# Attention of 16 heads: probabilities computed a second time with keys in rows, in place of transposes

## The chip, the core and the metric

The kernel runs on one core of a Trainium2 chip, in one launch. The metric is the device time of one execution in microseconds (us), as the median of several. The profile shown is one execution taken by the hardware profiler; its own time is given beside its span.

The engines are named as in the profile: PE (TensorE; PEld is its weight loads), DVE (VectorE), ACT (ScalarE), POOL (GpSimd), and SP, which only issues DMAs here. Matrix products write to PSUM, whose eight banks hold 512 float32 columns each.

## The reference

The input x has 32 sequences of 128 tokens with 128 features. Twelve residual layers follow each other, each with a layer normalization in front. The change concerns the fourth and the fifth. Both have 16 heads of 8 features. In the fourth, the keys and values are 8 features shared by all heads, and attention is causal. In the fifth, keys and values come from a context of the same shape, and a mask of 0 and 1 per key hides some keys.

```python
# fourth layer
latent = x @ Wc_down
q = (latent @ Wq_up).reshape(Bsz, Tlen, N_HEAD, HEAD_DIM)
kv = latent @ Wkv_up
k, v = (kv[..., :HEAD_DIM], kv[..., HEAD_DIM:])
att = jnp.einsum('bthd,bsd->bhts', q, k) * (1.0 / np.sqrt(HEAD_DIM))
att = jnp.where(causal[None, None], att, -jnp.inf)
att = jax.nn.softmax(att, axis=-1)
y = jnp.einsum('bhts,bsd->bthd', att, v).reshape(Bsz, Tlen, C)
return y @ Wc_proj

# fifth layer: q, k, v = query @ Wq.T + bq, keys @ Wk.T + bk, values @ Wv.T + bv, split into heads
energy = jnp.einsum('bhqd,bhkd->bhqk', q, k)
energy = jnp.where(mask[:, None, None, :] == 0, jnp.float32(-1e+20), energy)
attention = jax.nn.softmax(energy / np.sqrt(HEAD_DIM), axis=-1)
out = jnp.einsum('bhqk,bhkd->bhqd', attention, v)
return out.transpose(0, 2, 1, 3).reshape(N, Lq, EMBED) @ Wo.T + bo
```

## The kernel before

The 32 sequences are 8 groups (`G`) of 4 (`J`). All activations stay on the chip. The function `attention16` (line 502) runs the fourth and the fifth layer (`layer3`, line 1283, and `layer4`, line 1326) in one loop of rounds; a round n handles one sequence j of a group g, so the first 32 rounds are the causal layer and the next 32 the masked one. The same function is used once more for a later layer (`layer7`), which the change leaves as it is.

For one sequence the stages are these. `scores` forms, for all 16 heads, the products of queries and keys, with queries in the partitions (rows) and keys in the columns. A head has only 8 features, so four heads lie in each group of 32 rows, and `expand_keys` (line 477) holds keys spread over four column blocks with zeros in the other heads' features. Four products of 32 rows and 512 columns, one for each row group, fill four PSUM banks. The causal or mask term is added by further bf16 products: 16 small corner products in the causal layer, four in the masked one. DVE takes the maximum over the keys of each half (8 heads, 1024 columns), subtracts it for 12 of the heads, and ACT takes exponentials; four heads get the maximum as ACT's bias instead. `transposes` (line 558) turns the 16 blocks of 128 x 128 probabilities over on PE, four to a bank, and ACT copies each bank to SBUF, so that the keys lie in the partitions. `weighted` (line 569) multiplies them by the values and by ones (for the denominators), in 32 products of 32 output rows; DVE divides. After a group's four sequences `project` (line 640) applies the output matrix and adds the result to x.

PSUM is handed out under three tags of two buffers each: `two` (two banks each), `ps` (one bank) and `acc` (one bank). `scores` takes both `two` buffers, `transposes` takes `ps`, `weighted` takes `acc`. In SBUF the 1 MB tiles `bbig` (4 buffers) hold the probabilities before and after turning.

Beside the rounds of one group the inputs of the next one or two are made in steps (`step`, line 586, resumes the generator `before` of the layer): normalization by `normed` (statistics on DVE, the rest on POOL), transposes of its result (`turned_over`), and products for keys, queries and values. In the causal layer the keys and queries are made by `late`, at the end of a round. The spreading of keys in `expand_keys` is four POOL operations.

Within `run` the wrapper `Ordered` keeps PE, ACT and DVE in the order in which the program issues their instructions; POOL and the DMAs are placed by the scheduler. The order of a round before is:

```python
transposes(n, 0); e = scores(n + 1); transposes(n, 1); e(0)
step(g + 1)            # and step(g + 2) where j == 2
e(1)
weighted(n - 1)
# late() where it waits; project for a finished group
```

Of the kernel before, what the change touches and what calls it, by code (L numbers as in the profile page):

```python
# [10 lines left out]
F32 = mybir.dt.float32  # L11
BF16 = mybir.dt.bfloat16
I32 = mybir.dt.int32
# [8 lines left out]
CBLS = 4  # L22
HALF = B * S // 2
G = 8
# [30 lines left out]
def constants():  # L55

    p = np.arange(128)
    c = Columns()
    c.add("ident", np.eye(128))
    c.add("upper", (p[:, None] <= p[None, :]) * 1.0)  # L60
    c.add("causal", np.where(p[None, :] > p[:, None], NEG, 0.0))
    c.add("ones4", np.broadcast_to(np.repeat(np.eye(4), 8, 1).reshape(1, -1), (128, 128)))

    head = p // 32 * 8 + p % 8
    c.add("spread", (head[:, None] == np.arange(256)[None, :] // 8) * (p[:, None] % 32 // 8 == 1) * 1.0)
    c.add("count", np.broadcast_to(np.arange(40), (128, 40)))
    c.add("row", p[:, None] * 1.0)
    c.add("hm16", (p[:, None] // 8 == np.arange(16)[None, :]) * 1.0)
    c.add("n4", (p[:, None] % 32 // 8 == np.arange(4)[None, :]) * 1.0)
    c.add("m4", (p[:, None] // 32 == np.arange(4)[None, :]) * 1.0)  # L70
    k = p % 32

    c.add("means", (p[:, None] // 32 == p[None, :] // 32) * (k[:, None] <= k[None, :]) / (k[None, :] + 1.0))
    c.add("minus", -1.0 * (k[:, None] == 0))
    for e in (4, 8, 16):
        i = np.arange(e)
        c.add(f"tri{e}", np.broadcast_to(((i[None, :] < i[:, None]) * 1.0).reshape(1, -1), (128, e * e)))
    c.add("ones", np.ones((128, 128)))
    c.add("nhalf", np.full((128, 4), -0.5))
    return c  # L80


# [120 lines left out]
def program(ctx, tc, cols, x, ctxt, mask, drop, dfirst, dsmall, dwide, drows, dunits, dexperts, dconst, drel, dwq, out):  # L203
# [16 lines left out]
    def two(shape=(128, 2, 512)):  # L220

        return pp.tile(list(shape), F32, tag="two", name="two", bufs=2)
# [10 lines left out]
    def gmid(shape=(128, 512), dtype=F32):  # L233
        return mid.tile(list(shape), dtype, tag="gmid", name="gmid", bufs=10)
# [4 lines left out]
    def small(*shape):  # L239
        n = int(np.prod(shape))  # L240
        return sm.tile([128, *shape], F32, tag=f"s{n}", name="s", bufs=4 if n < 128 else 2)
# [6 lines left out]
    def mm(o, lhsT, rhs, start=True, stop=True):  # L248
        T.matmul(o, lhsT=lhsT, rhs=rhs, start=start, stop=stop)
# [22 lines left out]
            V.tensor_copy(o, p)  # L272


    cs = const.tile([128, cconst.n], F32, name="cs")
    K = {n: cconst.view(cs, n) for n in cconst.at}
    ident = K["ident"]
    xg = []
    for i in range(G):
        t = const.tile([128, J, D], F32, name=f"x{i}")  # L280
        SY.dma_start(out=t, in_=x[i * J : i * J + J].rearrange("b s d -> s b d"))
        xg.append(t)
        if i == 0:
            SY.dma_start(out=cs, in_=dconst)
            w0 = units.tile([128, cfirst.n], F32, tag="unit", name="w0")
            A.dma_start(out=w0, in_=dfirst)
            ww = const.tile([128, cwide.n], F32, name="ww")
            A.dma_start(out=ww, in_=dwide.to_broadcast([128, cwide.n]))
            wr = const.tile([1, crows.n], F32, name="wr")
            A.dma_start(out=wr, in_=drows)  # L290
# [18 lines left out]
    identb = const.tile([128, 128], BF16, name="identb")  # L309
    V.tensor_copy(identb, ident)  # L310

    acausal = const.tile([128, 64], BF16, name="acausal")
    V.tensor_copy(acausal, W0["acausal"])
    flip = const.tile([128, 128], BF16, name="flip")
# [162 lines left out]
    def expand_keys(w, src, bias=None):  # L477

        o = gbig((128, 4, 512))
        p, k = ps(), bmid()  # L480
        mm(p, w, src)
        if bias is None:
            A.copy(k, p)
        else:
            A.activation(k, p, AF.Identity, bias=bias)
        for n in range(4):
            P.tensor_scalar(o[:, n, :], k, K["n4"][:, n : n + 1], None, ALU.mult)
        return o
# [13 lines left out]
    def attention16(*layers):  # L502
# [108 lines left out]
        def go_round(n, others, then):  # L611
            g, j = n // J, n % J
            e = None
            if n < groups * J:
                transposes(n, 0)
            if n + 1 < groups * J:
                e = scores(n + 1)
            if n < groups * J:
                transposes(n, 1)
            if e:  # L620
                e(0)
            step(g + 1)
            if j == 2:
                step(g + 2)
            if g + 1 >= groups or (j == 3 and g + 2 == groups):
                next(then, None)
            if e:
                e(1)
            if 0 < n <= groups * J:
                weighted(n - 1)  # L630
            if g + 1 < groups and "late" in held[g + 1]:
                held[g + 1].pop("late")()
            next(others, None)
            if n > 1 and (n - 2) % J == J - 1:
                done = (n - 2) // J
                project(done % G, outs.pop(done), *layers[done // G][3:5])

        return lead(), run

    def project(i, yT, wo, bo):  # L640

        p = ps((128, J, 128))
        for j in range(J):
            mm(p[:, j, :], yT[:, j * 128 : (j + 1) * 128], wo)
        if bo is not None:
            P.tensor_tensor(xg[i], xg[i], bc(bo, 1, J), ALU.add)
        add_x(i, p)

    def linearT(w, src, bias=None, scale=1.0):

        p = ps()
        mm(p, w, src)
        o = gmid()
        if bias is not None:
            A.activation(o, p, AF.Identity, bias=bias, scale=scale)
        else:
            A.mul(o, p, scale)
        return o
# [623 lines left out]

    def layer3():

        rows, past = gmid((128, 4, 128)), sm.tile([128, 4, 128], BF16, tag="cbl", name="past", bufs=CBLS)
        _, at, n = cconst.at["causal"]
        for r in range(4):
            SY.dma_start(out=rows[32 * r : 32 * r + 32], in_=dconst[:, at : at + n].rearrange("(a p) k -> p a k", p=32))
        V.tensor_copy(past, rows)

        def extra(i, j, r):
            at = slice(32 * r, 32 * r + 32)
            return [(slice(32 * a, 32 * a + 32), identb[at, at], bc(past[at, a], 1, 4)) for a in range(4)]

        def before(i, h):
            xn = normed(i)
            yield
            xnT = turned_over(xn)
            yield
            p = ps()  # L1300
            mm(p[0:64, :], W["a1_down"], xnT)
            lat = gmid((64, 512))
            A.copy(lat, p[0:64, :])

            def late():
                h["k"] = expand_keys(W["a1_k"], lat)
                h["q"] = linearT(W["a1_q"], lat)

            if i:
                h["late"] = late  # L1310
            yield
            if i == 0:
                late()
            yield
            v = values_tile()
            pv, f = ps((128, J, 8)), small(J, 8)
            for j in range(J):
                mm(pv[:, j, :], lat[:, j * 128 : (j + 1) * 128], W["a1_v"])
            A.copy(f, pv)
            P.tensor_copy(diagonal(v)[:, 0:J], bc(f, 2, 4))  # L1320
            h["v"] = lambda j, r, n: flat(v[:, j, n])

        return before, 8**-0.5, extra, W["a1_o"], None, None, (1, 0, 0, 0)


    def layer4():
        masks = {}
        V.tensor_scalar(W["L1_xattn_bq"], W["L1_xattn_bq"], 8**-0.5, None, ALU.mult)

        def before(i, h):  # L1330
            mi = gmid((128, J * S), I32)
            SY.dma_start(out=mi, in_=mask[i * J : i * J + J].rearrange("b s -> (b s)").unsqueeze(0).to_broadcast([128, J * S]))
            xn = normed(i)
            yield
            mb = masks[i] = gmid((128, J * S), BF16)
            V.tensor_scalar(mb, mi, 0.0, -1e20, ALU.is_equal, ALU.mult)
            xnT = turned_over(xn)
            yield
            h["k"] = expand_keys(W["x1_Wk"], ctxT[i], W["x1_bk"])
            yield  # L1340
            h["q"] = linearT(W["x1_Wq"], xnT, W["L1_xattn_bq"], 8**-0.5)
            yield
            h["v"] = head_values(ctxT[i], W["x1_Wv"], WW["L1_xattn_bv"])

        def extra(i, j, r):
            row = slice(32 * r, 32 * r + 1)
            return [(slice(0, 128), onesb[row, :], bc(masks[i][row, j * S : (j + 1) * S], 1, 4))]

        return before, 1.0, extra, W["x1_Wo"], WW["L1_xattn_bo"], None, (1, 0, 0, 0)


    def layer5():
# [865 lines left out]
    lead2, run2 = layer2()  # L2218
    run1(rest0, lead2)
    load_units(6, 7)  # L2220
    lead3, run3 = attention16(layer3(), layer4())
    run2(lead3)
    lead5, run5, last6 = layer5()
    run3(iter(()), lead5)
# [39 lines left out]
```

## Time and profile before

| What | Value |
|---|---|
| Time, three runs | 2785.57, 2786.37, 2797.83 us; median 2786.37 |
| The profiled execution | 2801.5 us, span 2799.7 us, mean granted PE clock 0.939 |
| Busy shares of the span | PE 87%, DVE 74%, ACT 54%, POOL 34% |
| First scores of the causal layer, last of the masked one | start at 1028.7 and 1486.1 us |

The time column of the views counts from the start of the span. A group of instructions is named by engine, operation, the tile written and the tiles read (buffer numbers left out), and the shapes. All instructions pass through one helper, so they have one line number, and tiles tell them apart: `two<-gbig,gmid` are the score products of both layers, `ps<-cs,bbig` the transposes, `acc<-bbig,val` and `acc<-bbig,cs` the weighted sums and denominators, `two<-past,identb` the causal corners, `two<-gmid,onesb` the mask's products, `ps<-ws,...` and `ps<-xnT,ws` the projections. A float32 product is two instructions, a transpose is one. After the bar stand busy time and the mean of one; overlapping instructions count once in the busy time. "idle" is the time that the engine stood before them, and the arrow names what ended it.

### The profile page before, as it was taken

To read this page: it belongs to the slowest core of one execution; us is meant where nothing else is said; L and a number is where in the kernel's file an instruction comes from. 1 tells how busy PE (TensorE), PEld (TensorE's weight loads), DVE (VectorE), ACT (ScalarE), POOL (GpSimd) and SP (SyncE) were. 2 spreads that over 40 slices of the span, in tenths; PEclk is the share of its full clock that TensorE was granted. 3 is DMA by queue.
4 is the path that set the end of the run, shared out by engine and by line. 5 is a ranking of instruction groups with operands and counts; after the bars stand their busy time and mean duration, and the time that the engine had idled before them with its cause. 6 is when DMAs were issued, how large, how long until landed. Compare 5 with 4: busy or idle time off the path is not lost.

```text
span 2799.7 us, 56299 instructions
## 1 busy us (share of the span) xinstructions
PE 2434.1 (87%) x22929; PEld 1586.5 (57%) x22948; DVE 2081.3 (74%) x4091; ACT 1512.7 (54%) x3394; POOL 945.0 (34%) x977
## 2 busy tenths in 40 slices
PE   5988989999979999999997999988778999866664
PEld 3565667777744446666664444445555688444443
DVE  6978868878888867888887555558896525898993
ACT  4656544444422237777774454467884334566663
POOL 3534452232310214335552011133441454143432
PEclk8978899999999999999999999989998999988876
DMA  3000000000000010000000000000002357000000
GB/s 121 2 2 2 6 21 9 5 9 4 1 24 1 1 34 2 6 10 10 11 5 16 0 1 1 0 1 2 2 13 78 106 195 251 15 23 12 23 12 19
DMA packets 51045, 73.83 MB, mean 26 GB/s; under 512 B 3905, under 2 KB 41538, under 8 KB 50658
## 3 DMA queue, kind: packets, MB, share of 16 engines
q1 hardware_dynamic: 47728, 61.63, 6.9%
q0 software_dynamic: 2624, 5.40, 0.5%
q8 instruction: 181, 2.97, 0.4%
q10 hardware_dynamic: 434, 3.21, 0.3%
q14 instruction: 78, 0.64, 0.1%
HBM read 57.33 MB, written 12.89 MB: 25 GB/s over the span
## 4 chain that ended last, share of the span: by engine, by line
PE 56%; DVE 29%; ACT 8%; issue 4%; POOL 2%; DMA 1%; SPq 0%; DVEq 0%; ACTq 0%; POOLq 0%
PE ps L191 23%; PE two L191 17%; PE acc L191 15%; DVE bbig L191 11%; DVE s L191 8%; ACT bbig L191 4%; DVE gmid L191 4%; DVE bmid L191 3%; ACT bmid L191 1%; POOL xn L191 1%; ACT gmid L191 1%; DVE x L191 1%; ACT xn L191 1%; POOL s L191 1%; DMA ys<-yt,at 0%
## 5 line engine op out<-in xcount | busy, mean ns | idle before, releaser
L191 PE MATMUL ps<-cs,bbig 128*128 128x128 f32 x2208 | 336.8, 290 | 84.3 <-ACT bbig L191 31.9
L191 PEld LDWEIGHTS ps<-cs,bbig 128*128 128x128 f32 x2208 | 250.7, 146 | 196.7 <-ACT bbig L191 94.2
L191 ACT COPY bbig<-ps 128x512 f32<-128x512 f32 x418 | 227.5, 583 | 187.7 <-PE ps L191 187.5
L191 DVE TENSOR_REDUCE s<-two 128x8 f32<-128x1024 f32 (+1 forms) x192 | 234.0, 1219 | 72.8 <-PE two L191 71.5
L191 PE MATMUL two<-xnT,u 128*128 128x512 f32 x512 | 257.5, 603 | 12.1 <-ACT bmid L191 5.5
L191 DVE TENSOR_TENSOR bbig<-bbig 128x1024 f32<-128x1024 f32 (+3 forms) x234 | 246.4, 1093 | 11.2 <-ACT bbig L191 9.2
L191 PE MATMUL acc<-bmid,u 128*128 128x512 f32 x416 | 216.0, 606 | 15.4 <-DVE bmid L191 14.1
L191 ACT ACTIVATE bbig<-two,s 128x256 f32<-128x256 f32 (+1 forms) x512 | 189.8, 419 | 21.1 <-DVE s L191 17.5
L191 DVE TENSOR_TENSOR bmid<-bmid,ps 128x512 f32<-128x512 f32 x192 | 129.9, 683 | 90.2 <-ACT bmid L191 70.5
L191 POOL TENSOR_SCALAR gbig<-bmid,cs 128x512 f32<-128x512 f32 x96 | 148.5, 1563 | 142.5 <-ACT bmid L191 142.5
L191 POOL TENSOR_TENSOR s<-s,cs 128x4 f32<-128x4 f32 x112 | 127.8, 1142 | 172.6 <-DVE s L191 164.2
L191 PE MATMUL two<-gbig,gmid 32*128 32x512 f32 (+1 forms) x1248 | 183.9, 563 | 0.0
L191 ACT ACTIVATE bbig<-bbig 128x512 f32<-128x512 f32 (+1 forms) x160 | 128.2, 801 | 68.2 <-DVE bbig L191 67.9
L191 PEld LDWEIGHTS two<-xnT,u 128*128 128x128 f32 x512 | 90.4, 189 | 114.7 <-issue 53.6
L191 ACT ACTIVATE bmid<-two 128x512 f32<-128x512 f32 x92 | 54.9, 597 | 171.6 <-PE two L191 163.7
L191 ACT ACTIVATE bmid<-two,ws 128x512 f32<-128x512 f32 x128 | 85.1, 686 | 104.4 <-PE two L191 104.2
L191 POOL TENSOR_TENSOR x<-x,ww 128x512 f32<-128x512 f32 x64 | 89.0, 1391 | 142.0 <-ACT xn L191 83.3
L191 PEld LDWEIGHTS acc<-bmid,u 128*128 128x128 f32 x416 | 75.0, 192 | 103.1 <-DVE bmid L191 47.5
L191 POOL TENSOR_TENSOR bbig<-bbig,s 128x1024 f32<-128x1024 f32 x32 | 60.6, 1893 | 213.3 <-PE two L191 152.7
L191 ACT ACTIVATE bbig<-bbig,s 128x128 f32<-128x128 f32 x384 | 118.7, 388 | 24.4 <-DVE s L191 24.4
L191 POOL TENSOR_TENSOR x<-x,xn 128x512 f32<-128x512 f32 x24 | 32.8, 1368 | 290.1 <-DVE xn L191 264.5
L191 DVE TENSOR_TENSOR bbig<-two,s 128x512 f32<-128x512 f32 (+1 forms) x128 | 122.6, 958 | 8.6
(300 smaller groups left out, 5728.0 us busy)
## 6 DMA issues: line engine op xcount, KB each, us to landing
we<-in_experts SPq DMA_DIRECT2D x36, 768.0 KB
u<-in_units SPq DMA_DIRECT2D x9, 768.0 KB
gmid<-in_ctx SPq DMA_DIRECT2D x16, 256.0 KB
x<-in_x SPq DMA_DIRECT2D x8, 256.0 KB
gmid<-in_mask SPq DMA_DIRECT2D x8, 256.0 KB
ys<-bbig SPq DMA_DIRECT2D x2, 1024.0 KB
gmid<-ys SPq DMA_DIRECT2D x8, 256.0 KB
gmid<-in_drop SPq DMA_DIRECT2D x8, 256.0 KB
```

The lines of the kernel that those rows point to most:

```text
L191: d = self.made = f(*args, **kwargs)
```

## The change

A new function `attention16_turned` replaces `attention16` for these two layers.

- `scores` still forms the products with queries in rows, but only for the maximum. DVE writes the negative maximum as two bf16 parts (a high and a low one), four copies each, in a tile of 128 x 128.
- `turn_shift` turns that tile over with one bf16 product, and ACT copies it.
- `probabilities` forms the scores again with keys in rows. In the causal layer these are four products of 512 columns, with queries that are spread over four blocks (`qx`), and 16 corner products; in the masked layer 16 products of 128 columns. Sixteen further bf16 products with `pick16` add the shift of each head. The four banks come from one `two`, one `ps` and one `acc` buffer. Three ACT instructions take exponentials out of PSUM straight into the tile that `weighted` reads. The mask of the fifth layer is a bias for each partition (`hidden`) in that instruction.
- The subtraction, the exponentials in rows, the 16 transposes and their four copies per sequence are gone.
- The order of a round, and the point at which the steps of later groups are resumed, are new: scores two rounds ahead, probabilities one round ahead.
- In the causal layer `late` spreads both keys and queries, eight POOL operations in place of four.
- The constants in HBM hold the causal mask twice (also turned over), and they are no longer loaded with the other constants.

```diff
+    c.add("pick16", (p[:, None] % 16 == 4 * (p[:, None] // 32) + np.arange(4)[None, :]) * 1.0)
+    c.kept = c.n
+    c.add("causal", np.where(p[None, :] > p[:, None], NEG, 0.0))
+    c.add("causalT", np.where(p[None, :] < p[:, None], NEG, 0.0))
...
+    def attention16_turned(*layers):
+
+        held, shifts, turned, outs, ahead = {}, {}, {}, {}, {}
+        groups = len(layers) * G
+        last = groups * J
+
+        def scores(n):
+
+            g, j = n // J, n % J
+            extra = layers[g // G][2]
+            qT, keys = held[g]["q"], held[g]["k"]
+            cols_j = slice(j * 128, (j + 1) * 128)
+            halves = [two((128, 2, 4, 128)) for _ in range(2)]
+            terms = [extra(g % G, j, r) for r in range(4)]
+            for r in range(4):
+                rows = slice(32 * r, 32 * r + 32)
+                mm(halves[r // 2][:, r % 2], qT[rows, cols_j], keys[rows, :, cols_j], True, not terms[r])
+            for r in range(4):
+                for at, lhsT, rhs in terms[r]:
+                    mm(halves[r // 2][at, r % 2], lhsT, rhs, False, True)
+            m, parts = small(16), small(64).bitcast(BF16).rearrange("p (c k h) -> p c k h", c=4, k=2)
+            for half in range(2):
+                V.tensor_reduce(m[:, 8 * half : 8 * half + 8], halves[half].rearrange("p r n k -> p (r n) k"), AX.X, ALU.max)
+            V.tensor_scalar(parts[:, :, 0, :], bc(m, 1, 4), -1.0, None, ALU.mult)
+            V.scalar_tensor_tensor(parts[:, :, 1, :], bc(m, 1, 4), -1.0, parts[:, :, 0, :], ALU.mult, ALU.subtract)
+            shifts[n] = parts.rearrange("p c k h -> p (c k h)")
+
+        def turn_shift(n):
+            p = ps((128, 128))
+            mm(p, shifts[n], identb)
+            shifts[n] = small(64).bitcast(BF16)
+            A.copy(shifts[n], p)
+
+        def probabilities(n):
+
+            g, j = n // J, n % J
+            _, scale, _, _, _, extra, bias = layers[g // G]
+            qT, keys, shift = held[g]["q"], held[g]["k"], shifts.pop(n)
+            cols_j = slice(j * 128, (j + 1) * 128)
+            pr = turned[n] = bbig((128, 16, 128))
+            pair, third, fourth = two((128, 2, 4, 128)), ps((128, 4, 128)), acc((128, 4, 128))
+            quarters = [pair[:, 0], pair[:, 1], third, fourth]
+            rows = [slice(32 * r, 32 * r + 32) for r in range(4)]
+            for r in range(4):
+                if extra:
+                    mm(quarters[r], held[g]["kT"][rows[r], cols_j], held[g]["qx"][rows[r], :, cols_j], True, False)
+            for r in range(4):
+                for at, lhsT, rhs in extra(r) if extra else ():
+                    mm(quarters[r][at], lhsT, rhs, False, False)
+            for k in range(4):
+                for r in range(4):
+                    if not extra:
+                        mm(quarters[r][:, k], keys[rows[r], k, cols_j], qT[rows[r], cols_j], True, False)
+                for r in range(4):
+                    mm(quarters[r][:, k], pick16[rows[r], k : k + 1].to_broadcast([32, 128]), shift[rows[r], :], False, not extra or k == 3)
+            for heads, src in ((slice(0, 8), pair.rearrange("p r n q -> p (r n) q")), (slice(8, 12), third), (slice(12, 16), fourth)):
+                if bias is None:
+                    A.activation(pr[:, heads], src, AF.Exp, scale=scale)
+                else:
+                    A.activation(pr[:, heads], src, AF.Exp, bias=bias(g % G, j), scale=scale)
+
...
+        def lead():
+            for _ in range(4):
+                step(0)
+                yield
+            step(0)
+            step(1)
+            yield
+            scores(0)
+            step(1)
+            turn_shift(0)
+            yield
+            probabilities(0)
+            scores(1)
+            turn_shift(1)
+            yield
+
+        def run(others, then):
+            follow(T, A, V)
+            for n in range(last + 1):
+                go_round(n, others, then)
+            for _ in then:
+                pass
+            follow()
+
+        def go_round(n, others, then):
+            g, j = n // J, n % J
+            if n + 2 < last:
+                scores(n + 2)
+            if n and j == 0:
+                done = g - 1
+                project(done % G, outs.pop(done), *layers[done // G][3:5])
+            step(g + 1)
+            if j >= 2:
+                step(g + 2)
+            if n >= last - 6:
+                next(then, None)
+            if n + 1 < last:
+                probabilities(n + 1)
+            if n < last:
+                weighted(n)
+            if n + 2 < last:
+                turn_shift(n + 2)
+            if g + 1 < groups and "late" in held[g + 1]:
+                held[g + 1].pop("late")()
+            next(others, None)
 
         return lead(), run
 
...
 
     def layer3():
 
-        rows, past = gmid((128, 4, 128)), sm.tile([128, 4, 128], BF16, tag="cbl", name="past", bufs=CBLS)
-        _, at, n = cconst.at["causal"]
-        for r in range(4):
-            SY.dma_start(out=rows[32 * r : 32 * r + 32], in_=dconst[:, at : at + n].rearrange("(a p) k -> p a k", p=32))
-        V.tensor_copy(past, rows)
-
-        def extra(i, j, r):
+        pasts = []
+        for name in ("causal", "causalT"):
+            rows, past = gmid((128, 4, 128)), sm.tile([128, 4, 128], BF16, tag="cbl", name="past", bufs=CBLS)
+            _, at, n = cconst.at[name]
+            for r in range(4):
+                SY.dma_start(out=rows[32 * r : 32 * r + 32], in_=dconst[:, at : at + n].rearrange("(a p) k -> p a k", p=32))
+            V.tensor_copy(past, rows)
+            pasts.append(past)
+
+        def corners(past, r):
             at = slice(32 * r, 32 * r + 32)
             return [(slice(32 * a, 32 * a + 32), identb[at, at], bc(past[at, a], 1, 4)) for a in range(4)]
 
...
             A.copy(lat, p[0:64, :])
 
             def late():
-                h["k"] = expand_keys(W["a1_k"], lat)
+                h["kT"] = linearT(W["a1_k"], lat)
                 h["q"] = linearT(W["a1_q"], lat)
+                h["k"], h["qx"] = gbig((128, 4, 512)), bbig((128, 4, 512))
+                for o, src in ((h["k"], h["kT"]), (h["qx"], h["q"])):
+                    for n in range(4):
+                        P.tensor_scalar(o[:, n, :], src, K["n4"][:, n : n + 1], None, ALU.mult)
 
             if i:
                 h["late"] = late
...
             P.tensor_copy(diagonal(v)[:, 0:J], bc(f, 2, 4))
             h["v"] = lambda j, r, n: flat(v[:, j, n])
 
-        return before, 8**-0.5, extra, W["a1_o"], None, None, (1, 0, 0, 0)
+        return before, 8**-0.5, lambda i, j, r: corners(pasts[0], r), W["a1_o"], None, lambda r: corners(pasts[1], r), None
 
 
     def layer4():
         masks = {}
+        mi32, mb32 = small(128).bitcast(I32)[0:B], small(64).bitcast(BF16)[0:B]
+        SY.dma_start(out=mi32, in_=mask)
+        V.tensor_scalar(mb32, mi32, 0.0, -1e20, ALU.is_equal, ALU.mult)
+        p, hidden = ps((128, B)), const.tile([128, B], F32, name="hidden")
+        mm(p, mb32, identb[0:B, 0:B])
+        V.tensor_copy(hidden, p)
         V.tensor_scalar(W["L1_xattn_bq"], W["L1_xattn_bq"], 8**-0.5, None, ALU.mult)
 
         def before(i, h):
...
             row = slice(32 * r, 32 * r + 1)
             return [(slice(0, 128), onesb[row, :], bc(masks[i][row, j * S : (j + 1) * S], 1, 4))]
 
-        return before, 1.0, extra, W["x1_Wo"], WW["L1_xattn_bo"], None, (1, 0, 0, 0)
+        return before, 1.0, extra, W["x1_Wo"], WW["L1_xattn_bo"], None, lambda i, j: hidden[:, i * J + j : i * J + j + 1]
 
 
     def layer5():
...
     lead2, run2 = layer2()
     run1(rest0, lead2)
     load_units(6, 7)
-    lead3, run3 = attention16(layer3(), layer4())
+    lead3, run3 = attention16_turned(layer3(), layer4())
     run2(lead3)
     lead5, run5, last6 = layer5()
     run3(iter(()), lead5)
```

More of the change, by code (lines that the diff above doesn't have):

```diff
@@ L60, in constants @@
     c.add("upper", (p[:, None] <= p[None, :]) * 1.0)
-    c.add("causal", np.where(p[None, :] > p[:, None], NEG, 0.0))
     c.add("ones4", np.broadcast_to(np.repeat(np.eye(4), 8, 1).reshape(1, -1), (128, 128)))
@@ L272, in evac @@
             V.tensor_copy(o, p)
-    cs = const.tile([128, cconst.n], F32, name="cs")
-    K = {n: cconst.view(cs, n) for n in cconst.at}
+    cs = const.tile([128, cconst.kept], F32, name="cs")
+    K = {n: cconst.view(cs, n) for n in cconst.at if cconst.at[n][1] < cconst.kept}
     ident = K["ident"]
@@ L283, in program @@
         if i == 0:
-            SY.dma_start(out=cs, in_=dconst)
+            SY.dma_start(out=cs, in_=dconst[:, 0 : cconst.kept])
             w0 = units.tile([128, cfirst.n], F32, tag="unit", name="w0")
@@ L310, in program @@
     V.tensor_copy(identb, ident)
+    pick16 = const.tile([128, 4], BF16, name="pick16")
+    V.tensor_copy(pick16, K["pick16"])
     acausal = const.tile([128, 64], BF16, name="acausal")
@@ L636, in go_round, with weighted, step @@
                 project(done % G, outs.pop(done), *layers[done // G][3:5])
+        return lead(), run
+    def attention16_turned(*layers):
[52 more added lines that the diff above has]
+                    A.activation(pr[:, heads], src, AF.Exp, bias=bias(g % G, j), scale=scale)
+        def weighted(n):
+            g, j = n // J, n % J
+            values, prT = held[g]["v"], turned.pop(n)
+            if j == 0:
+                outs[g] = gmid()
+            yd = acc((128, 2, 128))
+            for side in range(2):
+                for k in range(4):
+                    for r in range(4):
+                        mm(yd[32 * r : 32 * r + 32, side], ones4[:, k * 32 : k * 32 + 32] if side else values(j, r, k),
+                           prT[:, 4 * r + k, :], k == 0, k == 3)
+            rec = small(128)
+            V.reciprocal(rec, yd[:, 1])
+            V.tensor_tensor(outs[g][:, j * 128 : (j + 1) * 128], yd[:, 0], rec, ALU.mult)
+            if j == J - 1:
+                held.pop(g)
+        def step(g):
+            if g < groups:
+                if g not in ahead:
+                    held[g] = {}
+                    ahead[g] = layers[g // G][0](g % G, held[g])
+                next(ahead[g], None)
+        def lead():
[21 more added lines that the diff above has]
+        def go_round(n, others, then):
+            g, j = n // J, n % J
+            if n + 2 < last:
[17 more added lines that the diff above has]
+            next(others, None)
@@ L1283, in layer3 @@
     def layer3():
-        rows, past = gmid((128, 4, 128)), sm.tile([128, 4, 128], BF16, tag="cbl", name="past", bufs=CBLS)
-        _, at, n = cconst.at["causal"]
-        for r in range(4):
-            SY.dma_start(out=rows[32 * r : 32 * r + 32], in_=dconst[:, at : at + n].rearrange("(a p) k -> p a k", p=32))
-        V.tensor_copy(past, rows)
-        def extra(i, j, r):
+        pasts = []
+        for name in ("causal", "causalT"):
+            rows, past = gmid((128, 4, 128)), sm.tile([128, 4, 128], BF16, tag="cbl", name="past", bufs=CBLS)
+            _, at, n = cconst.at[name]
+            for r in range(4):
+                SY.dma_start(out=rows[32 * r : 32 * r + 32], in_=dconst[:, at : at + n].rearrange("(a p) k -> p a k", p=32))
+            V.tensor_copy(past, rows)
+            pasts.append(past)
+        def corners(past, r):
             at = slice(32 * r, 32 * r + 32)
```

## The prediction

> **What bounds the kernel now.** First the page's head: the core's TensorE (PE) is busy for most of the span and no other engine comes near.
>
> ```profile
> span 2799.7 us, 56299 instructions
> PE 2434.1 (87%) x22929; PEld 1586.5 (57%) x22948; DVE 2081.3 (74%) x4091; ACT 1512.7 (54%) x3394; POOL 945.0 (34%) x977
> ```
>
> That is an average over twelve layers, so I looked at the changed layers alone. The starts of the score products in the timeline repeat every 4 rounds: 29.5 us per group in the causal layer, 27.9 us in the masked one. The windows over one such group each (columns: length, then busy us of PE, PEld, DVE, ACT, POOL, then clock) read:
>
> ```profile
> 1114.59:1144.12 29.53, 28.11 (x444) 18.64 (x443) 23.61 (x37) 21.29 (x45) 11.39 (x13) 1.00 0.01 2
> 1400.19:1428.08 27.89, 26.14 (x394) 18.16 (x393) 23.86 (x38) 21.32 (x44) 15.54 (x20) 1.00 0.02 7
> ```
>
> PE is busy 95% and 94%; DVE 80% and 86%, ACT 72% and 76%. The clock is granted in full. Next the chain that ended last, for one round of the masked layer:
>
> ```profile
> 1406.84 1.29 PE two L191 x12
> 1408.13 0.60 PE ps L191 x4
> 1408.76 0.59 ACT bbig L191
> 1409.35 0.04 issue
> 1409.39 1.16 PE ps L191 x8
> 1410.55 1.88 PE acc L191 x64
> 1412.43 1.02 PE ps L191 x8
> 1413.46 1.29 PE two L191 x12
> ```
>
> The round is PE's own queue: scores 1.29, eight transposes (part of them shown as 0.60, with an ACT copy of 0.59 that frees a bank), a projection of the next group 1.16, weighted sums 1.88, eight transposes 1.02. So only what changes on PE, or makes PE wait, counts.
>
> **What leaves.** The relevant groups, from the lists by shape of the masked layer (31 rounds) and, after the dots, of the causal one (28 rounds):
>
> ```profile
> L191 PE MATMUL ps<-cs,bbig 128*128 128x128 f32 x504 | 70.4, 280 | 5.1 <-ACT bbig L191 5.1
> L191 ACT COPY bbig<-ps 128x512 f32<-128x512 f32 x125 | 67.4, 584 | 31.3 <-PE ps L191 31.3
> L191 DVE TENSOR_TENSOR bbig<-two,s 128x1024 f32<-128x1024 f32 x31 | 37.9, 1224 | 1.1
> L191 PEld LDWEIGHTS two<-gbig,gmid 32*128 32x128 f32 x248 | 9.7, 182 | 5.2 <-issue 3.8 <-DVE gmid L191 1.2 <-DVE s L191 0.2
> L191 PEld LDWEIGHTS <-onesb 1*128 1x128 bf16 x124 | 3.5, 93 | 7.0 <-issue 7.0
> ...
> L191 PE MATMUL two<-past,identb 32*32 32x512 bf16 x448 | 12.2, 384 | 0.0
> ```
>
> Per round go 16 transposes (70.4/31 = 2.3 us of PE, plus about 0.2 of waiting for the copies), four ACT copies (2.2 us), DVE subtractions of 1024 and 512 columns (1.9 us). DVE and ACT get slack, which is worth nothing by itself; PE gets 2.4 us a round.
>
> **What PE gets instead.** Masked layer: 16 score products of 128 columns, two instructions each, so 32, in four row groups at once, and 16 bf16 picks of the shift. Rows of this size (transposes, projections) run at the pace of their weight loads, so I price them by the loads: 9.7/248 = 39 ns a load when four row groups overlap, 45 with a gap: 32 x 0.045 = 1.4 us. The picks: 3.5/124 = 28 ns, with a gap 31: 16 x 0.031 = 0.5. Together 1.9 us. Bounds: by pure streaming (scores of 512 columns take 1.07 us for the same columns) plus 0.2 for the picks, 1.3; with every item at 1.4 times my price, 2.6. The middle is nearest to the load rows. Causal layer: four products of 512 columns as in the first scores, 1.07; 16 corner products, 0.36 from start to start (12.2/28 = 0.44 busy); picks 0.5; sum 1.95, bounds 1.65 and 2.4. The product that turns the shift: one of 128 columns, 0.13 like a transpose. So on PE alone the exchange is 2.4 for 2.0: a gain of 0.4 us a round. It does not stay.
>
> [...]
>
> **The new wait.** PSUM has two `two` buffers. scores(n+2) takes both, and probabilities(n+1), behind it on PE, needs one back: PE must wait until DVE has reduced the first half. Rows for that:
>
> ```profile
> 1116.14 1.23 DVE L191 TENSOR_REDUCE s<-two 128x8 f32<-128x1024 f32 x1 [2.19 <-PE two L191]
> ...
> 1414.77 1.22 DVE L191 TENSOR_REDUCE s<-two 128x8 f32<-128x1024 f32 x1 [0.93 <-PE two L191]
> ```
>
> The scores before them began at 1114.59 and 1413.39, so the bank is free 1.55 + 1.23 + 0.07 = 2.85 us after the start of scores (causal), 2.7 (masked). PE has scores (1.43; 1.29) and that round's projection step to fill this. Weighted sums, 1.88, would have filled it but stand behind it. In the old order transposes stood there. ACT's exponentials (1.06 + two of 0.63) end under the weighted sums and the next scores, and DVE's reciprocal and product (1.25) under the next scores: no wait there.
>
> **Sum per group of four rounds.** What follows probabilities' start is P + 1.9 + 0.13: masked 3.9, causal 3.95.
> Rounds j=1 and 2: masked 2.7 + 3.9 = 6.6 each (a step of 1.1 fits in the wait; before, 6.6). Causal 2.85 + 3.95 = 6.8.
> Round j=0: project and a step, 1.05 each, end at 3.4 to 3.5; then probabilities wants a `ps` bank. Either the step's, copied by ACT at about 4.2, or project's, which DVE's add frees behind both reductions, two shift operations (0.2 each, like other small rows) and its own 0.69: about 5.0. Middle 4.6. Masked 4.6 + 3.9 = 8.5 (before 8.47). Causal: half of the scores run ahead (0.5 less) and `late` costs 1.98 as before: 4.6 + 3.45 + 2.0 = 10.05 (before 10.28).
> Round j=3: the transposes of the next input move one round closer to its normalization. POOL's rows:
>
> ```profile
> 1407.20 0.23 POOL L191 TENSOR_SCALAR s<-s 128x4 f32<-128x4 f32 x1 [1.58 <-DVE s L191]
> 1407.51 1.04 POOL L191 TENSOR_TENSOR s<-s,cs 128x4 f32<-128x4 f32 x1
> 1408.66 3.12 POOL L191 TENSOR_SCALAR xn<-x,s 128x128 f32<-128x128 f32 x4
> ...
> 1112.00 6.19 POOL L191 TENSOR_SCALAR gbig<-bmid,cs 128x512 f32<-128x512 f32 x4 [8.96 <-ACT bmid L191]
> ```
>
> From the first to the end of the third, 4.6 us. DVE's statistics start behind the shift operations, 4.3 into j=2, and end at 5.5; POOL ends at 10.1, that is 3.5 into j=3; transposes to 3.9, then 3.9: 7.8 (before 6.2). Causal: the second spread of four, 6.19 us more on POOL, starts behind the first (kT copied at 9.65 after the start of j=0) and ends at 22.05, 5.2 into j=2; with the values 6.0; normalization to 10.6, 3.8 into j=3; 4.2 + 3.95 = 8.15 (before 6.4). The first spread ends at 15.9, before scores of the next group at 16.85, so it hides, with 1 us to spare.
> Masked: 6.6 + 6.6 + 8.5 + 7.8 = 29.5 against 27.9, +1.6; times 8 is +13. Causal: 6.8 + 6.8 + 10.05 + 8.15 = 31.8 against 29.5, +2.3; times 8 is +18. Start and end: the second scores can follow the first sooner, about 2 us (the old first round stood 3.4 us for exponentials), and one drain round goes, about 2: -4. The additional setup (four 64 KB DMAs, a mask DMA, a cast of 0.43, some small operations) is queued near 770 us, where the cast of the first mask ran at 774.6 under another layer's PE work: 0, or 1 to 2 if uncovered. SP has no other change in the loop.
> Total 13 + 18 - 4 = +27 us: the profiled execution would go from 2801.5 to 2828; it lies 15 above the median of 2786.4, and on the median I get 2813.
>
> **Rivals.**
> Slower, forecast: waits and moved steps take back more than PE's exchange gives, 2813.
> Faster: PE's queue alone counts. If a bank comes back in time (the scheduler's allocation, a prompter DVE) and P is at its low end, masked gives 2.4 - 1.3 - 0.13 = 1.0 a round, causal 2.4 - 1.65 - 0.13 = 0.6: 32 x 1.6 + 4 = 55, so 2731. It decides where PE shows no wait on DVE before probabilities, that is below 1.4 us of uncovered reduction. Against it: the reduction rows end 1.4 us after PE is through its scores. Half of that gain, 2759, would count here too.
> No change: low prices (1.3; 1.65) and the early `ps` bank, with the waits: three of four rounds shorten by 0.6 and 0.3, j=0 by 0.4: masked -2.2, causal -1.3 per group, 8 x 3.5 = 28 off: 2785.
> Much slower: 128-column loads do not overlap. By the transposes' load row (107 ns), 48 loads take 5.1 us: +3.2 x 32 = 102 in the masked layer, 2915.
>
> **How the numbers follow.** A measurement of this kernel tells 0.5% (14 us) from no change. Forecast 0.60, faster 0.13, no change 0.22, much slower 0.05. Low end: between 2759 and 2785, since the faster rival is cut, 2766. High end: prices 2.6 and 2.4 add 3 x 0.7 + 3 x 0.45 = 3.45 a group, 28; the late bank 0.45 x 16 = 7: 2848, and 2852 with the setup uncovered.
>
> **What would show it.** Right: before probabilities, PE idle behind DVE `s` (the reduction) in j=1 and 2 of the causal layer, about 1.4 us, and behind POOL `xn` in j=3; groups of about 31.8 and 29.5 us; ACT under 55% and DVE under 70% busy there, PE under 90%. Wrong: groups shorter than 29.5 and 27.9 with PE above 94% (the waits are hidden); or PE still full and longer (then the price of the 128-column products was too low).

## The result

| Kernel | Median | Runs |
|---|---|---|
| before | 2788.49 us | 2785.57 to 2797.83 |
| changed | 2831.42 us | 2829.93 to 2835.53 |

The ratio is 1.015, with a 95% interval of 1.0123 to 1.0178: the change makes the kernel 43 us slower by the medians. The profiled executions differ by less, 34.0 us in span (2833.7 against 2799.7), because the one of before lies 13 us above its median and the one of the changed kernel 4 us. The first product of the later layer's positions (`ps<-rels,flip`) starts at 1613.0 us instead of 1576.7, 36.3 us later, so the whole loss arises ahead of it, in the two changed layers.

The head of the changed kernel's page; the columns are as before:

```profile
span 2833.7 us, 59541 instructions
PE 2457.0 (87%) x24805; PEld 1571.3 (55%) x24805; DVE 2002.6 (71%) x4031; ACT 1362.0 (48%) x3008; POOL 999.8 (35%) x1009
```

DVE lost 79 us of work and ACT 151 us, and nothing was won by it. The windows over one group of each layer (length, then PE, PEld, DVE, ACT, POOL, clock):

```profile
1112.45:1143.81 31.36, 28.18 (x543) 15.28 (x542) 18.23 (x34) 11.58 (x22) 17.52 (x16) 1.00 0.01 2
1402.63:1433.38 30.75, 28.11 (x525) 19.55 (x524) 18.51 (x35) 12.36 (x21) 15.68 (x20) 0.89 0.04 11
```

The causal group takes 31.36 us (29.53 before), with nearly the same busy time of PE (28.18 and 28.11). The masked one takes 30.75 (27.89 before), and there the granted clock is 0.89 and no longer 1.00. The chain that ended last, over the rounds j=1 and j=3 of a masked group, shows both waits:

```profile
1402.70 1.33 PE two L194 x12
1404.03 1.22 DVE s L194
1405.29 0.38 PE two L194 x2
...
1406.84 1.89 PE acc L194 x65
...
1410.23 2.35 DVE s L194 x2
1412.60 0.43 DVE s L194
1413.05 1.49 DVE s L194 x9
...
1416.09 3.14 POOL xn L194 x4
1419.27 0.48 PE ps L194
...
1422.51 3.12 PE acc L194 x65
```

In j=1 DVE's reduction (`DVE s`, 1.22) now stands in the chain between the scores and the second scores. From j=2 into j=3 the chain leaves PE for 9 us (1410.23 to 1419.27): reductions, shift operations and statistics on DVE, then normalization on POOL. And the weighted sums behind that take 3.12 us where they took 1.89 before. The clock in windows of a few us around that place says why:

```profile
1411.40:1414.80 3.40, 3.31 (x112) 3.02 (x112) 3.06 (x12) 2.28 (x4) 1.88 (x5) 1.00 0.01 2
1414.80:1418.20 3.40, 2.24 (x23) 0.80 (x15) 3.04 (x4) 0.70 (x2) 3.21 (x5) 1.00 0.02 5
1418.19:1425.02 6.83, 6.22 (x100) 5.07 (x104) 1.33 (x4) 2.86 (x4) 3.43 (x5) 0.50 0.00 0
1425.00:1426.00 1.00, 1.00 (x29) 0.72 (x21) 0.29 (x1) 0.17 (x1) 0.00 (x1) 0.99 0.08 16
```

After a stretch in which PE was busy for 2.24 of 3.40 us, the clock falls to 0.50 and stays there from 1418.19 to 1425.02. In the causal layer, whose wait is the same kind:

```profile
1125.26 0.70 PE L194 MATMUL two<-bbig,gmid 32*128 32x512 f32 x2 [1.33 <-DVE s L194]
...
1127.03 1.08 PE L194 MATMUL acc<-bbig,val 128*32 128x128 f32 x32
```

PE stood 1.33 us for the reduction in j=1, and the second scores with corners and shift took 1.77 us from the first line to the second.

### The profile page after: what moved, and what is told of

The parts are those of the page before. It is cut to its first block, busy times and chain, and to the rows that moved or that the text cites. A ratio compares the mean times of both kernels' runs of the same rounds, so it can differ in the third digit from the quotient of the medians.

```text
span 2833.7 us, 59541 instructions
## 1 busy us (share of the span) xinstructions
PE 2457.0 (87%) x24805; PEld 1571.3 (55%) x24805; DVE 2002.6 (71%) x4031; ACT 1362.0 (48%) x3008; POOL 999.8 (35%) x1009
## 4 chain that ended last, share of the span: by engine, by line
PE 55%; DVE 29%; ACT 6%; POOL 5%; issue 3%; DMA 1%; SPq 0%; ACTq 0%; DVEq 0%; POOLq 0%
PE ps L194 20%; PE two L194 20%; PE acc L194 16%; DVE s L194 10%; DVE bbig L194 10%; DVE gmid L194 4%; DVE bmid L194 3%; POOL xn L194 3%; ACT bbig L194 2%; ACT bmid L194 1%; POOL s L194 1%; DVE x L194 1%; ACT gmid L194 1%; ACT xn L194 1%; DMA ys<-yt,at 1%
## 5 line engine op out<-in xcount | busy, mean ns | idle before, releaser
L194 PE MATMUL ps<-cs,bbig 128*128 128x128 f32 x1184 | 185.9, 293 | 71.4 <-ACT bbig L194 21.8
L194 PEld LDWEIGHTS ps<-cs,bbig 128*128 128x128 f32 x1184 | 137.3, 147 | 135.5 <-ACT bbig L194 51.5
L194 DVE RECIPROCAL s<-acc 128x128 f32<-128x128 f32 x96 | 91.5, 953 | 166.2 <-PE acc L194 166.2
L194 ACT COPY bbig<-ps 128x512 f32<-128x512 f32 x162 | 89.2, 582 | 117.7 <-PE ps L194 117.7
L194 ACT ACTIVATE bbig<-two 128x1024 f32<-128x1024 f32 x96 | 94.7, 1020 | 95.9 <-PE acc L194 71.0
L194 ACT ACTIVATE bbig<-two,s 128x256 f32<-128x256 f32 x256 | 118.1, 477 | 20.5 <-DVE s L194 20.5
L194 PE MATMUL acc<-bbig,val 128*32 128x128 f32 x3072 | 116.6, 298 | 2.8 <-ACT bbig L194 2.8
```

The lines of the kernel that those rows point to most:

```text
L194: d = self.made = f(*args, **kwargs)
```

## The experiments

The theory: PE waits (for a bank that DVE's reduction frees, and for the normalization that its transposes now follow one round sooner), and these waits, with the clock that falls behind the second, make the loss. The rival: the second score products cost PE more than the transposes did. All ratios are to the kernel before.

**The normalization one round earlier**, all else as changed:

```diff
-            if j >= 2:
+            if j in (1, 3):
                 step(g + 2)
```

> The changed kernel, but the normalization of group g+2 is started in round j=1 and turned over in round j=3, so POOL has one round more. Theory (waits of PE, above all the one on POOL's normalization in j=3 and the low clock behind it, make the loss): round j=3 falls from 10.7 to about 6.3 us in the masked layer and from 8.1 to about 6.7 in the causal one, so 8 x 4.4 + 8 x 1.5 = 47 us less than the changed kernel, near 2785. Rival (the added products cost PE more than the transposes did): the rounds j=1 and 2 and the time stay, within 5 us of 2831. In the causal layer POOL also spreads keys and queries (12.4 us a group), so half of its 1.5 may be lost.

Measured 2797.87 us against 2793.76 beside it, ratio 1.0004 (0.9983 to 1.0025). The loss is gone, and the products are all still there, so the rival falls. All masked rounds but j=0 take 6.20 us now, up to the last ones. One group of the masked layer:

```profile
1392.87:1419.12 26.25, 24.64 (x525) 17.30 (x524) 19.07 (x35) 12.23 (x21) 15.42 (x20) 1.00 0.04 13
```

The exchange has not become free everywhere: a masked group is 1.6 us shorter than in the kernel before (26.25 for 27.89), and a causal one still 1.4 longer (30.95 for 29.53), and the two cancel. The causal j=3 fell only from 8.08 to 7.67 (one of them took 9.17, 1.5 us more; the three groups of the changed kernel in which the clock stood at 0.50 for 3.41 us were longer by as much); the chain there, from one j=0 to the next j=3, names POOL, as the second half of the expectation allowed:

```profile
1120.47 6.19 POOL gbig L194 x4
1126.66 6.16 POOL bbig L194 x4
...
1134.24 3.13 POOL xn L194 x4
...
1137.41 0.33 PE ps L194
```

**The wait filled.** Two products of the identity ahead of each transpose, in both layers, into columns that the transpose overwrites; the order stays that of the change:

```diff
 for j in range(J):
+    for _ in range(2):
+        mm(p[:, j * 128 : (j + 1) * 128], ident, ident)
     turn_over(p[:, j * 128 : (j + 1) * 128], xn[:, j, :])
```

> The changed kernel with two float32 products (128 columns, identity by identity) ahead of each transpose of the normalized input in both layers, into columns that the transpose then overwrites. They add no wait where PE waits for POOL anyway. Theory (the low granted clock after round j=3 comes from PE standing idle there): the clock stays at 1.00, probabilities and weighted sums of that round take 1.5 and 1.9 us and not 2.75 and 3.1 us, masked groups shorten by about 2.5 us and three of the causal ones by 1.5: 25 us less, near 2806. Rival (the clock falls for another reason, such as load or time): no change or 2 to 5 us more.

Measured 2810.21 us, ratio 1.0046 (1.0025 to 1.0066): 0.0104 less than the changed kernel, 29 us. PE does more and the kernel is faster. The same round j=3 of a masked group:

```profile
1427.95:1435.99 8.04, 8.03 (x149) 5.95 (x146) 4.36 (x7) 3.02 (x6) 6.58 (x8) 1.00 0.01 2
```

It takes 8.04 us instead of 10.7 with the clock at 1.00. So of the changed kernel's 43 us about 29 come from the clock, and the rest of what the earlier normalization wins back, about 12 us, from the wait itself.

**The reduction of the first half twice**, on the kernel with the earlier normalization:

```diff
+            V.tensor_reduce(m[:, 0:8], halves[0].rearrange("p r n k -> p (r n) k"), AX.X, ALU.max)
             for half in range(2):
```

> The kernel with the earlier normalization, and the maximum of the first half taken twice (1.22 us more on DVE per round, the same result). Theory (PE waits each round for the first reduction to free a bank of the two-buffer tag): rounds j=1, 2 and 3 grow by 1.2 us each in both layers, j=0 by 0 to 0.5: 8 x 3.9 + 8 x 3.6 = 60 us more than with the earlier normalization alone. Rival (DVE is 60% busy and has slack, PE's queue sets the round): within 10 us of it.

Measured 2896.60 us, ratio 1.0349 (1.0309 to 1.0389), some 96 us more than without it. The undisturbed rounds grew as the theory said, from 6.20 to 7.6 and from 6.65 to 8.0 us. Others reach 9.1 to 10.8 us, which the expectation did not have: behind the longer wait the weighted sums in the chain take 3.52 us for 1.89. The first 32 of their products take 1.94 us, as in the changed kernel at the clock of 0.50, where at 1.00 they take 1.08.

```profile
1408.70 1.22 DVE s L194
1409.94 1.24 DVE s L194
1411.18 0.14 issue
...
1412.86 3.52 PE acc L194 x65
```

In the kernel with the earlier normalization DVE is busy for 59% of a causal group and 73% of a masked one (19.07 of 26.25 us). It sets the round all the same, since PE waits for it inside the round.

**Weighted sums ahead of the second scores**, again with the earlier normalization:

```diff
-            if n + 1 < last:
-                probabilities(n + 1)
             if n < last:
                 weighted(n)
+            if n + 1 < last:
+                probabilities(n + 1)
```

> The kernel with the earlier normalization, and weighted(n) ahead of probabilities(n+1) on PE, so that 1.88 us of work stand in the wait for the reduction. The second half of scores then needs the bank whose exponentials end 1.1 us after the round begins, and weighted needs all exponentials, 2.2 us after it. Theory: causal rounds j=1 to 3 fall from 6.65 to about 5.9, j=0 by 0.6; masked rounds j=1 to 3 grow by 0.2: about 20 us less than with the earlier normalization alone. Rival (the wait only changes its name, ACT takes DVE's place): within 5 us of it.

Measured 2833.38 us, ratio 1.0140 (1.0104 to 1.0177), 38 us more instead of 20 less. My expectation was wrong, and worse than the rival named beside it. The wait changed its name: scores, now directly behind the second scores, need the banks that ACT's exponentials read.

```profile
1129.47 2.21 PE L194 MATMUL two<-gbig,gmid 32*128 32x512 f32 x8
...
1146.35 3.06 PE L194 MATMUL ps<-gmid,ws 64*128 64x512 f32 x4 [1.50 <-ACT bbig L194]
```

The scores take 2.21 us and not 1.14, and at the end of j=0 `late` waits 1.5 us more for a `ps` bank and then takes 3.06 us for the 1.98 of the kernel before, and the weighted sums behind it 2.84 for 1.89: 13.0 us for that round. The weighted sums did fill the wait, as the prediction remarked: no wait for DVE stands ahead of the second scores here. It was worth nothing, since the wait for ACT took its place.

**The moved step alone, in the kernel before.** The transposes of the normalized input in j=3, an empty step in j=0, and the start adapted to it:

```diff
-            if j == 2:
+            if j == 2 or (j == 3 and len(layers) == 2):
                 step(g + 2)
...
             xnT = turned_over(xn)
             yield
+            yield
```

> The kernel before, with only one part of the change: the transposes of the normalized input are issued in round j=3, one round after the normalization is started, instead of two; nothing else of the steps moves. Theory (the moved step is a loss by itself, whatever replaces the transposes of the probabilities): PE reaches that step about 2.5 us before POOL ends, in nearly all of 14 groups, 30 to 40 us more than before, and more where the clock falls behind the wait. Rival (the loss belongs to the second score products): within 8 us of before.

Measured 2814.57 us against 2790.27, ratio 1.0090 (1.0069 to 1.0110), 25 us: a little under the expected 30 to 40, and far from the rival's 8. The chain of a masked group, and the windows over that group:

```profile
1420.72 1.07 DVE s L191 x8
...
1423.33 3.15 POOL xn L191 x4
...
1426.53 0.33 PE ps L191
```

```profile
1391.94:1421.44 29.50, 27.01 (x393) 18.40 (x392) 24.50 (x40) 21.37 (x45) 15.75 (x19) 1.00 0.03 11
```

The chain leaves PE for the same statistics and the same normalization as in the changed kernel, but the clock stays at 1.00. So in the masked layer the wait alone costs 1.6 us a group here (29.50 for 27.89). In the causal layer 32 products of the weighted sums took 1.57, 1.95 and 1.96 us in three places (at 1087.8, 1185.0 and 1248.8), which at the clock of 1.00 take 1.06 to 1.08: there it fell.

**Queries spread on ACT**, with the earlier normalization:

```diff
-                        P.tensor_scalar(o[:, n, :], src, K["n4"][:, n : n + 1], None, ALU.mult)
+                for n in range(4):
+                    A.mul(h["qx"][:, n, :], h["q"], K["n4"][:, n : n + 1])
```

> The kernel with the earlier normalization, and the spreading of queries (four operations a group in the causal layer) on ACT instead of POOL. Theory (in the causal layer POOL's queue, 6.2 + 6.2 + 4.6 us, now sets round j=3): that round falls from 7.67 to about 6.65 us, and the start loses its 1.7 us wait for POOL: 8 to 10 us less than the earlier normalization alone. Rival (POOL's place in the chain is hidden, ACT's added 2.4 us delays the exponentials): 0 to 5 us more.

Measured 2782.93 us, ratio 0.9977 (0.9961 to 0.9993): 7.5 us less than the earlier normalization alone. The two intervals overlap, but the round shows the gain: causal j=3 takes 6.65 us for 7.67. At the start the wait for POOL is gone, yet from the first scores to the sixth it takes 43.5 us for 42.6.

**And the queries' product in the step of j=1**, out of `late`:

```diff
-                h["q"] = linearT(W["a1_q"], lat)
...
             if i == 0:
                 late()
+            h["q"] = linearT(W["a1_q"], lat)
             yield
```

> As the kernel with the earlier normalization and the queries spread on ACT, and the product for the queries is taken out of the end of round j=0 and put in the step of round j=1, where PE waits 1.3 us for the first reduction. Theory: causal rounds j=0 fall by about 1.0 us, j=1 stays at 6.65, so 8 us less than without the move; groups of about 28.9 and 26.3 us against 29.5 and 27.9 before: 5 + 13 us less than before, a ratio near 0.994. Rival (the wait for the reduction is not free time, or the start eats the gain): no faster than before.

Measured 2778.81 us, ratio 0.9962 (0.9944 to 0.9979): 0.4% less than the kernel before, though not clear of the version above. The round j=0 fell by 0.86 us, but j=1 rose from 6.65 to 7.1, since the keys' spread on POOL now ends after PE wants it. One run more tried to take that back, with one of the four spreads of the keys on ACT, and the same kernel as above beside it:

> As the version with the queries' product in round j=1, and one of the four spreads of the keys on ACT, so that POOL needs 4.7 us for the rest and not 6.2. Theory (the round j=1 of 7.1 us there is PE at the next scores waiting for POOL's spread of keys): that round falls to 6.65, 8 x 0.45 = 4 us less, a ratio to before near 0.995. Rival (the wait is another one): no change against it, 0.996.

> The version with the queries' product in round j=1 a second time, beside the one with the shared spread on the same chip, for a comparison within one set of runs: a ratio to before near 0.996.

The round j=1 did fall, to 6.65 us, and j=2 rose to 6.73. The times do not tell the two apart: 0.9964 (0.9947 to 0.9981) and 0.9963 (0.9949 to 0.9978).

## Why the prediction was right, and where it was off

- **Direction and mechanism** were right: PE's gain per round is taken back by the wait for the reduction, and by the moved step. 2813 was forecast and 2831 measured; for the profiled execution 2828 against 2835.5.
- **The wait for the reduction**: about 1.4 us was forecast in the causal j=1 and j=2; 1.33 was found in j=1, and 0.34 in j=2, where PE has products of 1.05 us for the next group's values to do meanwhile. The causal rounds were 9.98, 6.65, 6.65 and 8.08 us; forecast were 10.05, 6.8, 6.8, 8.15. Three of the first seven groups were 1.5 us longer by the clock (0.50 for 3.41 us), and the eighth, beside which the masked layer begins, 1.6 (9.23 us for j=3, and 7.63 with the wait filled).
- **The price of the second scores**: causal 1.77 us for 1.95. Masked 1.49 (from the first second-score product to the first weighted sum, 1405.29 to 1406.78) for 1.9, near the streaming bound of 1.3. Pricing the small products by 45 and 31 ns for each load was too dear: 48 of them in 1.49 us are 31 ns each. The 5.1 us of the rival "much slower" (48 loads one behind the other, at the 107 ns of busy time for each of the transposes' loads before: 46.3 us for 432 of them) did not come: the 32 loads of the score products last 185 ns each, 5.9 us together, and all lie within the 1.49 us, so these loads overlap. So the masked j=1 and 2 took 6.20 for 6.6.
- **The bank in j=0**: the earlier of the two came, with ACT's copy; PE waited 0.42 us, and the masked j=0 took 7.66 for 8.5.
- **The moved step in j=3** is the term that was mis-sized: 7.8 us in the masked layer, and 10.7 measured. The wait itself was 0.8 us longer than forecast (second scores at 4.7 us into the round, not 3.9: POOL ended 4.2 us into it and not 3.5, and the last transposes ran at the low clock, 0.48 us for 0.33). The larger part, 2.5 us, is the half clock over second scores (2.77 us for 1.49) and weighted sums (3.1 for 1.9). The prediction had read the clock as 1.00 in both layers and kept it; it did not ask what a new idle stretch does to it. The filled wait shows it: there the round took 8.04 us, near the 7.8.
- **Sum**: masked +2.85 a group for +1.6, causal +1.85 for +2.3 (with the clock about +2.4). **Start and end**: -4 was forecast. From the sixth scores to the last, 58 of the 64 rounds, the profile shows +36.3 us; ahead of that the start costs 3 (PE waits 1.66 us for POOL's spread of queries, and the clock stays at 0.50 for 17.1 us, before for 6.8), and the end gives 3 back, so 0.
- **Luck**: errors of both signs meet in the total. In the masked layer j=0, 1 and 2 were forecast 1.6 us a group too long, and j=3 2.9 too short. With the wait filled, which leaves the clock at 1.00, a masked group takes 28.10 us for the 29.5 forecast, and the kernel loses 0.46%, about 13 us and not 27. So what the prediction reasoned out is worth about half of its figure; that the figure came near the measured one it owes in part to the fall of the clock, which it did not have.
- **Signs**: DVE (58% and 60%) and ACT (37% and 40%) were as low as named. PE was named under 90%, and was busy 90% of a causal group and 91% of a masked one, where the low clock makes its products longer.
- **Rivals**: the faster one needed PE without these waits. With the earlier normalization a masked group takes 26.3 us against 27.9, 0.4 us a round of the 1.0 that this rival named; the wait for the reduction stays, and the best version is 0.4% faster and not 2%. The rival of no change had prices (1.3 and 1.65) and a bank nearer to what came than the forecast had; j=3 and the clock stood against it. Much slower did not occur.

What stays open: what brings the clock down in one wait and not in the next. The causal layer has the same kind of wait in every group and lost the clock in three of its first seven. The busy share alone does not decide it, as two stretches below show.

## What to carry to other kernels

Work taken off engines with slack (79 us of DVE, 151 us of ACT) was worth nothing here while the bound engine's own queue got no shorter, and a tag with two buffers tied that queue to an engine that is 59% to 73% busy: 1.22 us more of its work in each of 64 rounds made the kernel 96 us slower. When a step is moved in an order written by hand, follow its inputs through every engine that makes them: here one moved line cost 25 us by itself, more than the whole exchange of transposes for products with that line put right. Where a change gives PE a new wait, look at the clock behind it, or fill the wait: in seven masked groups of the changed kernel the work behind 1.6 to 1.8 us of waiting for POOL ran at 0.50, and with products in that wait at 1.00.

## What the runs showed of the hardware

The granted clock fell to 0.50 for 6.8 us though PE was busy for two thirds of the 3.4 us before, and products without use in that wait kept it at 1.00 and made the kernel 29 us faster. In the masked layer it fell in every group, and four of these falls were 30.7 us apart (1326.0, 1356.8, 1387.5, 1418.2), where a group takes 30.75 us; in the causal layer it fell for 3.41 us at 1076.9, 1172.4 and 1268.0, so 95.6 us apart. The busy share ahead of a fall does not decide it alone. Two stretches of the causal layer, of 3.41 us each:

```profile
1073.45:1076.86 3.41, 2.06 (x26) 0.78 (x26) 2.35 (x4) 0.59 (x1) 1.98 (x3) 1.00 0.00 0
1090.51:1093.92 3.41, 2.08 (x29) 0.47 (x27) 1.29 (x2) 1.01 (x2) 2.90 (x2) 1.00 0.00 0
```

PE was busy for 2.06 us in the first and 2.08 in the second; behind the first the clock fell, behind the second it stayed at 1.00.

DVE's two small shift operations took 0.20 and 0.22 us in most rounds, and 0.42 and 0.41 where POOL's `val` products ran beside them (1412.60 to 1413.46, the products from 1412.10). Beside other work of POOL it was otherwise: beside its spread of keys they took 0.20 and 0.22 (from 1221.97), beside its spread of queries in the causal layer the second took 0.66.
